# An attention stage with 16 small heads: values made once and spread over DRAM, two-bank scores, outputs issued behind scores

## The chip, the cores and the metric

The kernel runs on one core of one Trainium2 chip. The metric is the device time of one execution in microseconds (us). The kernel before was run three times: 1251.08, 1251.42 and 1253.64 us, median 1251.42 us.

## What is computed

The input is x of 4 sequences of 1024 tokens of 128 features. Two blocks follow each other, each with an attention part and a feed-forward part behind a modulated layer norm. Block 0 has a linear attention and a mixture of 16 small experts. Block 1 has the attention that the change is about, and then a two-layer local transformer as its feed-forward part ("block 2" below). Block 1's attention, shortened:

```python
H, W, PREFIX = 16, 64, 16                  # 16 heads of 8 features
qc = q.reshape(B, H, C, W, 8)              # chunks of 64 queries
kt, vt = the 128 keys and values that end with each chunk (zeros ahead of the start)
sg = einsum('bhcqd,bhkd->bhcqk', qc, k[:, :, :PREFIX]) / sqrt(8)
st = einsum('bhcqd,bhckd->bhcqk', qc, kt) / sqrt(8)
mg = arange(PREFIX) <= q_pos
mt = (diff >= 0) & (diff < W) & (kt_pos >= PREFIX)        # diff = q_pos - kt_pos
scores = concatenate([where(mg, sg, -1e9), where(mt, st, -1e9)], -1)
out = einsum('bhcqk,bhckd->bhcqd', softmax(scores, -1), concatenate([vg, vt], 3))
x = x + ga * (out_as_tokens @ w_out.T)
```

So each query sees the 16 prefix keys and the last 64 keys.

## The kernel before

Activations are kept transposed (`xT`, `hT`: 128 features on the partitions, 1024 tokens along the row), one tile for each of the four sequences b. Block 1's attention works on tiles of 128 queries, 8 for each sequence, 32 in all. A query block has 32 queries and sees three key blocks of 32 (96 keys) and the prefix, so a row has 4 heads x 112 = 448 scores in one PSUM bank, and 4 banks (j = 0 to 3) hold the 16 heads.

For one tile the steps are:

- `scores` (L249): for each of the 4 banks a bf16 matmul writes the mask (identity times the mask constants `mks`, L255); 16 matmuls add the window scores, of which four run on separate row groups of the array (L261); 4 add the prefix scores (L270).
- `weights` (L713): on VectorE (DVE) the negated maximum of each bank (`maximum`, L279) and, for banks 0 to 2, an add of it (L722); on ScalarE (ACT) the exponential. Bank 3 is read by ACT straight from PSUM, one exponential for each head with the maximum as bias (L726). Each bank's result is an SBUF tile `pr`.
- `flip` (L728): TensorE (PE) transposes the 4 heads of a bank into a PSUM tile of tag "t" (two buffers), ACT copies it to SBUF (`pt`, L735).
- `values` (L692): GpSimd (POOL) copies the four overlapping windows of `hT` and the prefix into `hr`; four fp32 matmuls project them (L708), ACT copies the result to `vb`, with a column of ones behind each head's 8 values.
- `outputs` (L739): 64 small matmuls into one half of the bank `obank` (L750, columns 0 to 143 for even tiles, 144 to 287 for odd ones), then on DVE the reciprocal of the sums (`rs`, L752) and the product (`on`, L754).
- `back` (L757): PE transposes `on` into the last 128 columns of the same bank (L760), ACT copies it to `os` (L763).

An fp32 matmul is two instructions in the profile, so 32 instructions on L261 are 16 matmuls.

PSUM has eight banks and all are used: "s" four (scores; block 0's `hidden` uses the same four), "t" two, "m" one (`values`, and in turn `queries`, `keys`, `tokens`, `normed`, `project_out`), "o" one (`obank`).

PE's instructions run in the order in which the program writes them; the other engines' are put in order by the planner ahead of the run, by the order of the program and by when it expects each to be ready. It also sets all waits. The loop over g (from -1 to 33, L792) is that written order: in step g it issues scores and weights of tile g+2, side work (`queries`, `tokens`, `normed` of some sequence), `back` of g-1, the first flip of g+1, values of g+1, outputs of g, the second flip of g+1, and in some steps `project_out`, `keys` and, from g = 26 on, the first projections of block 2 (L651). `tokens` transposes half a sequence into "m" and computes a layer norm's statistics, `normed` transposes it back and writes `hT`.

Block 0's `hidden` (L483) makes two products `h` of 512 columns for each pair of experts; ACT takes the first through silu (`u`), POOL multiplies `u` by the routing weights, DVE multiplies by the second (`g`); `mixed` sums the experts' outputs.

The weights of block 2 (L601 to L613) are loaded by DMAs on SyncE's (SP's) queue at the start of block 1's attention.

Of the kernel before, what the change touches and what calls it, by code (L numbers as in the profile page):

```python
# [19 lines left out]
F32 = mybir.dt.float32  # L20
# [6 lines left out]
P = 128  # L27
# [6 lines left out]
H0 = 16  # L34
# [14 lines left out]
def adaln_blocks(ctx: ExitStack, tc: tile.TileContext, a: dict, out: bass.AP):  # L49
# [199 lines left out]
    def scores(b, t):  # L249
        nt = f"{b}_{t}"  # L250
        q1, kx, kg = kept1[b, "q"], kept1[b, "kx"], kept1[b, "kg"]
        S = [ps.tile([P, 512], F32, tag="s", name=f"s_{nt}_{j}", bufs=4) for j in range(4)]
        sv = [x[:, 0 : 4 * (W3 + PREFIX)].rearrange("p (h k) -> p h k", h=4) for x in S]
        for j in range(4):
            pe.matmul(sv[j], lhsT=identb, rhs=mks[:, min(t, 1), :].unsqueeze(1).to_broadcast([P, 4, W3 + PREFIX]), start=True, stop=False)  # L255
        for a in range(4):
            i = 4 * t + a
            lo = max(0, 2 - i)
            for j in range(4):
# [6 lines left out]
                    stop=False,  # L266
                )
        for j in range(4):
            rw = slice(32 * j, 32 * j + 32)
            pe.matmul(sv[j][:, :, W3:], lhsT=q1[rw, t * P : (t + 1) * P], rhs=kg[rw, 4 * j : 4 * j + 4, :], start=False, stop=True)  # L270
        mx = pre.tile([P, H0], F32, tag="mx", name=f"mx_{nt}", bufs=3)
        kept1[b, t, "s"] = sv, mx
        if (b, t) == (0, 0):
            for j in range(4):
                maximum(b, t, j)

    def maximum(b, t, j):
        sv, mx = kept1[b, t, "s"]
        dve.tensor_reduce(mx[:, 4 * j : 4 * j + 4], sv[j], AX.X, ALU.max, negate=True)  # L279


# [3 lines left out]
    with (  # L285
# [184 lines left out]
        def shared_hidden(b):  # L470

            hh = []
            for i in range(2):
                h = ps.tile([P, BLK], F32, tag="s", name=f"hs{i}_{b}", bufs=4)
                for k in range(NB):
                    pe.matmul(h[k * INTER : (k + 1) * INTER, :], lhsT=ws13[:, i, :], rhs=hT[b][:, blk(k)], start=True, stop=True)
                hh.append(h)
            u = wp.tile([P, BLK], F32, tag="u", name=f"us_{b}")
            act.activation(u, hh[0], AF.Silu)
            g = kept[b, "gs"] = wb.tile([P, BLK], F32, tag="gs", name=f"gs_{b}")  # L480
            dve.tensor_tensor(g, u, hh[1], ALU.mult)

        def hidden(b, k, c):  # L483

            nm = f"{b}_{k}_{c}"
            hh = []
            for w in (w1, w3):
                h = ps.tile([P, BLK], F32, tag="s", name=f"h_{nm}", bufs=4)
                pe.matmul(h, lhsT=w[:, c * P : (c + 1) * P], rhs=hT[b][:, blk(k)], start=True, stop=True)  # L489
                hh.append(h)  # L490
            u = wp.tile([P, BLK], F32, tag="u", name=f"u_{nm}")
            act.activation(u, hh[0], AF.Silu)  # L492
# [3 lines left out]
            dve.tensor_tensor(g, u, hh[1], ALU.mult)  # L496
# [104 lines left out]
    wl = []  # L601
    for l in range(DEPTH):
        w = [const1(f"wqkv_{l}", [P, 3, HEADS * DH]), const1(f"wo_{l}", [P, 4, D]), const1(f"w1_{l}", [P, 2 * HID]), const1(f"w2_{l}", [P, 3, D])]
        nc.sync.dma_start(out=w[0], in_=a["wqkv"][l].rearrange("p (i c) -> p i c", i=3))
        nc.sync.dma_start(out=w[1], in_=a["wo"][l].rearrange("(c p) d -> p c d", p=P))
        nc.sync.dma_start(out=w[2], in_=a["mw1"][l])
        for j, r in enumerate(CH):
            nc.sync.dma_start(out=w[3][:r, j, :], in_=a["mw2"][l][j * P : j * P + r, :])
        wl.append(w)

    abs_ = [const1(f"ab_{l}", [P, 2, NT, 2, DH]) for l in range(DEPTH)]
    tab = abs_[DEPTH - 1]
    nc.sync.dma_start(out=tab, in_=a["tab"])  # L613
# [70 lines left out]
    with (  # L684
        tc.tile_pool(name="w6o", bufs=1) as wo6,
# [4 lines left out]
        odd.append(wo6)  # L690

        def values(b, t):  # L692

            nt = f"{b}_{t}"
            hr = wp.tile([P, 4, KV], F32, tag="hr", name=f"hr_{nt}", bufs=2)
            c0 = 2 if t == 0 else 0
            win = hT[b][:, (4 * t + c0 - 2) * KB :]
            win = bass.AP(tensor=win.tensor, offset=win.offset, ap=[win.ap[0], [KB, 4 - c0], [1, W3]])
            pool.tensor_copy(hr[:, c0:, 0:W3], win)
            if t == 0:  # L700

                pool.memset(hr[:, 0:2, 0 : 2 * KB], 0.0)
# [519 lines left out]
```

## Time and profile before

| | |
|---|---|
| median of three runs | 1251.42 us |
| span of the profiled execution | 1254.1 us |
| its total beside the span | not given apart |
| PE, DVE, ACT, POOL busy in the span | 1167.7, 879.4, 812.7, 812.2 us |
| granted TensorE clock, mean | 0.977 |
| first scores of block 1 (L255) | 324.70 us |
| masks of g = 1 and of g = 26 start | 346.92, 539.03 us |
| first work of block 2 behind the stage (L843) | 588.78 us |

The block 1 attention is thus the stretch from about 325 to 589 us. A line of the profile's timeline gives the start, the time from the first start to the last end of a merged group, engine, line of the kernel, operation, what is written and read, the shapes and the count, and in brackets how long the engine stood idle before it and whom it waited for. Instructions on one engine overlap: what a group costs is the distance from its start to the next group's start. PE is matmul time, PEld the loading of weights, which runs beside it.

### The profile page before, as it was taken

To read this page: it belongs to the slowest core of one execution; us is meant where nothing else is said; L and a number is where in the kernel's file an instruction comes from. 1 tells how busy PE (TensorE), PEld (TensorE's weight loads), DVE (VectorE), ACT (ScalarE), POOL (GpSimd) and SP (SyncE) were. 2 spreads that over 40 slices of the span, in tenths; PEclk is the share of its full clock that TensorE was granted. 3 is DMA by queue.
4 is the path that set the end of the run, shared out by engine and by line. 5 is a ranking of instruction groups with operands and counts; after the bars stand their busy time and mean duration, and the time that the engine had idled before them with its cause. 6 is when DMAs were issued, how large, how long until landed. Compare 5 with 4: busy or idle time off the path is not lost.

```text
span 1254.1 us, 34759 instructions
## 1 busy us (share of the span) xinstructions
PE 1167.7 (93%) x13578; PEld 717.7 (57%) x13578; DVE 879.4 (70%) x2806; ACT 812.7 (65%) x2215; POOL 812.2 (65%) x805
## 2 busy tenths in 40 slices
PE   6788989998899999988898999999999999999998
PEld 5544444543476667665565555656655556566564
DVE  5656263452466666675879888888899888898864
ACT  3362362322477677775787777788878777788862
POOL 4445443745434353534789988988889889888840
PEclk9798999998999999999999999999999999999999
DMA  6040403022300000000111111111111111111110
GB/s 177 1 137 1 137 0 117 20 70 66 135 4 4 3 20 4 20 4 3 27 36 40 26 39 27 35 39 27 39 27 26 39 30 40 48 27 31 36 39 26
DMA packets 36136, 51.04 MB, mean 41 GB/s; under 512 B 5850, under 2 KB 17668, under 8 KB 35844
## 3 DMA queue, kind: packets, MB, share of 16 engines
q1 hardware_dynamic: 35540, 48.29, 14.3%
q8 instruction: 107, 1.75, 0.6%
q10 hardware_dynamic: 432, 0.53, 0.1%
q14 instruction: 57, 0.47, 0.1%
HBM read 26.52 MB, written 2.36 MB: 23 GB/s over the span
## 4 chain that ended last, share of the span: by engine, by line
PE 44%; DVE 25%; ACT 18%; POOL 6%; issue 6%; DMA 1%; POOLq 0%; ACTq 0%; SPq 0%; DVEq 0%
PE h L489 4%; ACT pr L902 4%; PE yp L949 4%; DVE pr L890 4%; DVE co L656 3%; DVE si L661 3%; PE s L883 3%; DVE ss L663 3%; PE ptr L733 3%; POOL u L494 3%; PE qk L651 3%; PE y L504 2%; PE s L261 2%; ACT sq L654 2%; PE obank L750 2%
## 5 line engine op out<-in xcount | busy, mean ns | idle before, releaser
L902 ACT ACTIVATE pr<-pr,mx 128x128 f32<-128x128 f32 x512 | 200.8, 403 | 87.8 <-DVE mx L890 87.7
L671 POOL TENSOR_TENSOR co<-co,si 128x512 f32<-128x512 f32 x123 | 156.5, 1278 | 80.3 <-DVE si L661 73.5
L667 POOL TENSOR_TENSOR ss<-ss,nhalf 128x16 f32<-128x16 f32 x64 | 191.2, 2987 | 5.3
L890 DVE CUSTOM_DVE_ANT_0 pr<-s,masks,ss 128x128 f32<-128x128 f32 x512 | 144.2, 345 | 42.2 <-PE s L883 40.9
L494 POOL TENSOR_TENSOR u<-u,cw 128x512 f32<-128x512 f32 x64 | 81.0, 1268 | 102.3 <-ACT u L492 100.0
L651 PE MATMUL qk<-wqkv,hs 128*128 128x512 f32 x256 | 137.7, 620 | 4.3 <-ACT pt L735 4.3
L496 DVE TENSOR_TENSOR g<-u,h 128x512 f32<-128x512 f32 x64 | 43.9, 686 | 127.2 <-POOL u L494 127.2
L489 PE MATMUL h<-hT,w 128*128 128x512 f32 x256 | 125.0, 612 | 0.4 <-DVE g L496 0.4
L279 DVE TENSOR_REDUCE mx<-s 128x4 f32<-128x448 f32 x128 | 73.6, 618 | 55.2 <-PE s L270 55.2
L492 ACT ACTIVATE u<-h 128x512 f32<-128x512 f32 x64 | 38.2, 597 | 112.8 <-PE h L489 111.3
L656 DVE TENSOR_TENSOR co<-qk,ab 128x512 f32<-128x512 f32 x128 | 87.1, 680 | 26.1 <-ACT sq L654 26.1
L902 ACT ACTIVATION_READ_ACCUMULATOR pr<-pr,mx 128x1 f32 x512 | 101.6, 198 | 0.0
L924 PEld LDWEIGHTS ptr<-ident,pr 128*128 128x128 f32 x512 | 63.6, 141 | 61.6 <-issue 55.1
L661 DVE TENSOR_TENSOR si<-qk,ab 128x512 f32<-128x512 f32 x128 | 87.0, 680 | 0.0
L663 DVE TENSOR_REDUCE ss<-sq 128x8 f32<-128x512 f32 x128 | 86.4, 675 | 0.0
L489 PEld LDWEIGHTS h<-hT,w 128*128 128x128 f32 x256 | 49.8, 198 | 63.8 <-issue 56.7
L654 ACT ACTIVATE sq<-qk 128x512 f32<-128x512 f32 x128 | 74.9, 585 | 14.7 <-PE qk L651 12.2
L843 PE MATMUL qktr<-ident,co 128*128 128x128 f32 x492 | 77.4, 281 | 6.6 <-POOL co L673 5.2
L883 PEld LDWEIGHTS s<-kT,qT 64*64 64x64 f32 x2048 | 56.1, 133 | 45.5 <-issue 22.1
L917 POOL TENSOR_TENSOR pr<-pr,sm 128x512 f32<-128x512 f32 x64 | 74.6, 1167 | 7.8 <-DVE sm L910 7.8
L735 ACT COPY pt<-ptr 112x512 f32<-112x512 f32 x128 | 72.6, 612 | 10.7 <-PE ptr L733 10.7
L883 PE MATMUL s<-kT,qT 64*64 64x128 f32 x2048 | 71.4, 275 | 7.6 <-DVE kT L856 6.1
(211 smaller groups left out, 2865.0 us busy)
## 6 DMA issues: line engine op xcount, KB each, us to landing
cw<-cd SPq DMA_DIRECT2D x128, 128.0 KB, 3.1
ve<-vs SPq DMA_DIRECT2D x120, 128.0 KB, 2.3
hs<-hT SPq DMA_DIRECT2D x16, 256.0 KB, 3.2
out<-out SPq DMA_DIRECT2D x7, 256.0 KB, 2.7
xin<-in_x SPq DMA_DIRECT2D x3, 512.0 KB, 6.1
w<-in_w SPq DMA_DIRECT2D x3, 512.0 KB, 5.9
wqkv<-in_wqkv SPq DMA_DIRECT2D x2, 768.0 KB, 5.3
ab<-in_tab SPq DMA_DIRECT2D x1, 1024.0 KB, 7.0
```

The costliest lines, as they stand in the source:

```text
L489: pe.matmul(h, lhsT=w[:, c * P : (c + 1) * P], rhs=hT[b][:, blk(k)], start=True, stop=True)
L494: pool.tensor_tensor(u, u, kept[b, k, "cw"][:, c, :], ALU.mult)
L651: pe.matmul(ps, lhsT=hs[l, b][:, t * P : (t + 1) * P], rhs=wl[l][0][:, w, :], start=True, stop=True)
L654: act.activation(sq, ph, AF.Square)
L656: dve.tensor_tensor(co, ph, abs_[l][:, 0, t, w, :].unsqueeze(1).to_broadcast([P, HEADS, DH]), ALU.mult)
L661: dve.tensor_tensor(si.rearrange("p h (i e) -> p h i e", i=2), ex, sn, ALU.mult)
L663: dve.tensor_reduce(ss[:, w, :], sq, AX.X, ALU.add)
L667: pool.tensor_tensor(ss, ss, nhalf[:, 0:2].unsqueeze(2).to_broadcast([P, 2, HEADS]), ALU.pow)
L671: pool.tensor_tensor(co, co, si, ALU.add)
L883: pe.matmul(S[j][qs, c, :], lhsT=q[rw, c, qs], rhs=k[rw, c, at : at + P], start=True, stop=True)
L890: dve.tensor_tensor_reduce(out=pr[:, c, :], in0=S[j][:, c, :], in1=mk[:, min(t, 1), :], scale=kept[l, b, t, "ss"][:, 0, h : h + 1], scalar ...
L902: act.activation(pr[:, c, :], pr[:, c, :], AF.Exp, bias=mx[:, j, c : c + 1], scale=-1.0, accum_out=sm[:, j, c : c + 1])
```

## The change

- `values` projects each token once (one matmul of 128 tokens for a tile), ACT copies it with the column of ones to `vt`, and DMAs on SP write it to a DRAM tile `dv`, read the four overlapping windows back into `vb` and the prefix rows four times. Zeros stand ahead of a sequence's start. It is issued two tiles ahead of `outputs`, not one.
- Masks are written to the first and third key block only (256 of 448 columns), except for the first tile of a sequence.
- Scores lie in two tiles of two banks. Banks 2 and 3 come first; DVE takes one maximum over two banks, one add for banks 0 and 1 together (`prw`), and one add for bank 2; ACT does bank 3's exponentials before the others.
- In the loop, `outputs` of g and the flip of banks 3 and 2 come straight behind the scores, ahead of side work; `back`, `values` and the flip of banks 0 and 1 follow.
- Block 0's `hidden` and `shared_hidden` take one two-bank tile where they took two one-bank tiles.
- Block 2's weights are loaded one piece a step, behind the window's DMA, from g = 1 on.

```diff
     def scores(b, t):
-        S = [ps.tile([P, 512], F32, tag="s", name=f"s_{nt}_{j}", bufs=4) for j in range(4)]
-        sv = [x[:, 0 : 4 * (W3 + PREFIX)].rearrange("p (h k) -> p h k", h=4) for x in S]
-        for j in range(4):
-            pe.matmul(sv[j], lhsT=identb, rhs=mks[:, min(t, 1), :].unsqueeze(1).to_broadcast([P, 4, W3 + PREFIX]), start=True, stop=False)
+        S = [ps.tile([P, 2, 512], F32, tag="s", name=f"s_{nt}_{i}", bufs=2) for i in range(2)]
+        sp = [x[:, :, 0 : 4 * KV].rearrange("p j (h k) -> p j h k", h=4) for x in S]
+        sv = [sp[j // 2][:, j % 2] for j in range(4)]
+        for j in (2, 3, 0, 1):
+            to, of = sv[j], mks[:, min(t, 1), :]
+            if t == 0:
+                of = of.unsqueeze(1).to_broadcast([P, 4, KV])
+            else:
+                to = to[:, :, 0:W3].rearrange("p h (c k) -> p h c k", k=KB)[:, :, 0:3:2, :]
+                of = of[:, 0:W3].rearrange("p (c k) -> p c k", k=KB)[:, 0:3:2, :].unsqueeze(1).to_broadcast([P, 4, 2, KB])
+            pe.matmul(to, lhsT=identb, rhs=of, start=True, stop=False)
...
+    def maximum(b, t, i):
+        sp, mx = kept1[b, t, "s"]
+        dve.tensor_reduce(mx[:, 8 * i : 8 * i + 8].rearrange("p (j h) -> p j h", j=2), sp[i], AX.X, ALU.max, negate=True)
...
         def hidden(b, k, c):
-            hh = []
-            for w in (w1, w3):
-                h = ps.tile([P, BLK], F32, tag="s", name=f"h_{nm}", bufs=4)
-                pe.matmul(h, lhsT=w[:, c * P : (c + 1) * P], rhs=hT[b][:, blk(k)], start=True, stop=True)
-                hh.append(h)
+            hh = ps.tile([P, 2, BLK], F32, tag="s", name=f"h_{nm}", bufs=2)
+            for i, w in enumerate((w1, w3)):
+                pe.matmul(hh[:, i], lhsT=w[:, c * P : (c + 1) * P], rhs=hT[b][:, blk(k)], start=True, stop=True)
...
         def values(b, t):
             if t == 0:
+                dv = kept1[b, "dv"] = dr1.tile([2 * KB + N, H0 * 9], F32, tag="dv", name=f"dv_{b}")
+                nc.sync.dma_start(out=dv[0 : 2 * KB], in_=zero)
+            dv = kept1[b, "dv"]
+            vp = ps.tile([P, BLK], F32, tag="m", name=f"vp_{nt}")[:, 0:D]
+            pe.matmul(vp, lhsT=hT[b][:, t * P : (t + 1) * P], rhs=wqkv1[:, 2, :], start=True, stop=True)
+            vt = wp.tile([P, H0, 9], F32, tag="vt", name=f"vt_{nt}")
+            pool.memset(vt[:, :, 8:9], 1.0)
+            act.copy(vt[:, :, 0:8], vp.rearrange("p (h e) -> p h e", e=8))
+            at = 2 * KB + t * P
+            nc.sync.dma_start(out=dv[at : at + P], in_=vt.rearrange("p h e -> p (h e)"))
+            v = kept1[b, t, "v"] = wp.tile([KV, 4, H0 * 9], F32, tag="vb", name=f"vb_{nt}")
+            win = dv[t * P : t * P + W3]
+            win = bass.AP(tensor=win.tensor, offset=win.offset, ap=[win.ap[0], [KB * H0 * 9, 4], win.ap[1]])
+            kept1["brought"] = nc.sync.dma_start(out=v[0:W3], in_=win)
+            nc.sync.dma_start(out=v[W3:KV], in_=dv[2 * KB : 2 * KB + PREFIX].unsqueeze(1).to_broadcast([PREFIX, 4, H0 * 9]))

         def weights(b, t):
-            for j in range(4):
+            wide = kept1[b, t, "pr", 0] = wp.tile([P, 2, 4, KV], F32, tag="prw", name=f"prw_{b}_{t}", bufs=2)
+            for i in (1, 0):
                 if (b, t) != (0, 0):
-                    maximum(b, t, j)
+                    maximum(b, t, i)
+                mi = mx[:, 8 * i : 8 * i + 8].rearrange("p (j h) -> p j h", j=2)
+                if i == 0:
+                    dve.tensor_tensor(wide, sp[0], bc(mi, [P, 2, 4, KV]), ALU.add)
+                    act.activation(wide, wide, AF.Exp)
+                    continue
+                pr = [wp.tile([P, 4, KV], F32, tag="pr", name=f"pr_{b}_{t}_{j}", bufs=4) for j in range(2)]
+                for h in range(4):
+                    act.activation(pr[1][:, h, :], sp[1][:, 1, h, :], AF.Exp, bias=mi[:, 1, h : h + 1])
+                dve.tensor_tensor(pr[0], sp[1][:, 0], bc(mi[:, 0], [P, 4, KV]), ALU.add)
+                act.activation(pr[0], pr[0], AF.Exp)
...
             when(g + 2, scores)
             when(g + 2, weights)
+            when(g, outputs)
+            when(g + 1, flip, (3, 2))
             if ahead and t in (2, 4):
                 queries(b + 1, t // 2 - 1)
...
             when(g - 1, back)
+            for i in {-1: (0, 1)}.get(g, (g + 2,)):
+                when(i, values)
             when(g + 1, flip, (0, 1))
-            when(g + 1, values)
-            when(g, outputs)
-            when(g + 1, flip, (2, 3))
+            if g > 0 and local_loads:
+                with tc.issue_after(kept1["brought"].ins):
+                    nc.sync.dma_start(out=local_loads[0][0], in_=local_loads[0][1])
+                del local_loads[0]
```

## The prediction

> **What bounds the kernel now.** I read the page first, then a table of stages, then the instructions of one step in order of time, then the waits. The page says that TensorE is busy nearly always, and the stage in question is no exception:
>
> ```profile
> PE 1167.7 (93%) x13578; PEld 717.7 (57%) x13578; DVE 879.4 (70%) x2806; ACT 812.7 (65%) x2215; POOL 812.2 (65%) x805
> 450.00:520.00 70.00, 67.09 (x1850) 48.51 (x1848) 47.18 (x113) 50.12 (x124) 35.78 (x59) 1.00 0.05 11
> ```
>
> The second line is a stretch in the middle of block 1's attention (stretch, its length, then busy us of PE, PEld, DVE, ACT, POOL, granted clock, DMA share, GB/s): PE 67.1 of 70 us, DVE 47, ACT 50, clock full, DMA idle. So PE work that goes away should shorten the step, up to the point where a chain through DVE or ACT is as long. One step without side work (g = 15) in the timeline of PE:
>
> ```profile
> 458.61 0.92 PE L255 MATMUL s<-cb,identb 128*128 128x448 bf16 x4
> 459.46 0.93 PE L261 MATMUL s<-kx,q 32*32 32x384 f32 x32
> 460.32 0.47 PE L270 MATMUL s<-kg,q 32*128 32x64 f32 x8
> 460.72 0.33 PE L760 MATMUL obank<-ident,on 128*128 128x128 f32 x1
> 460.88 1.04 PE L733 MATMUL ptr<-ident,pr 128*112 128x128 f32 x8
> 461.75 1.04 PE L708 MATMUL vp<-wqkv,hr 128*112 128x128 f32 x8
> 462.72 1.26 PE L750 MATMUL obank<-vb,pt 112*32 112x9 f32 x128
> 463.91 1.09 PE L733 MATMUL ptr<-ident,pr 128*112 128x128 f32 x8
> 464.83 0.73 PE L255 MATMUL s<-cb,identb 128*128 128x448 bf16 x3
> ```
>
> Start to start this costs: masks 0.85, windows 0.86, prefix 0.40, `back` 0.16, first flip 0.87, values 0.97, outputs 1.19, second flip 0.92; 6.22 in all, no gap. DVE in the same step:
>
> ```profile
> 460.79 1.16 DVE L279 TENSOR_REDUCE mx<-s 128x4 f32<-128x448 f32 x2 [1.91 <-PE s L270]
> 461.86 1.15 DVE L722 TENSOR_TENSOR pr<-s,mx 128x448 f32<-128x448 f32 x2
> 462.92 1.15 DVE L279 TENSOR_REDUCE mx<-s 128x4 f32<-128x448 f32 x2
> 463.98 0.62 DVE L722 TENSOR_TENSOR pr<-s,mx 128x448 f32<-128x448 f32 x1
> 464.51 0.25 DVE L752 RECIPROCAL rs<-obank 128x16 f32<-128x16 f32 x1
> 464.80 0.29 DVE L754 TENSOR_TENSOR on<-obank,rs 128x128 f32<-128x128 f32 x1
> ```
>
> To be seen: DVE starts as soon as the scores are done, does all seven big operations of `weights` (0.53 each, start to start), and only then `rs` and `on` of `outputs`, because `weights` is earlier in the program. `on` ends 4.37 us after PE left the scores (460.72). Nobody minds now: `back` uses `on` one step later.
>
> Two more pairs of lines matter. At the end of the stage:
>
> ```profile
> 582.61 0.26 ACT L763 COPY os<-obank 128x128 f32<-128x128 f32 x1
> 583.01 1.17 PE L750 MATMUL obank<-vb,pt 112*32 112x9 f32 x102 [0.82 <-ACT os L763]
> ```
>
> The outputs of tile 31 write columns 144 to 287 of the bank `obank`; the copy of tile 30 reads columns 384 to 511. They share no element, and still PE waited 0.82 us for the copy: accesses of two engines to one bank are put in program order. And:
>
> ```profile
> 468.06 0.78 ACT L161 ACTIVATE hT<-out_h,mod 128x512 f32<-128x512 f32 x1 [1.38 <-PE out_h L160]
> 468.88 0.93 PEld L708 LDWEIGHTS vp<-wqkv,hr 128*112 128x112 f32 x8 [0.19 <-ACT hT L161]
> ```
>
> The bank "m" exists once: values wait until ACT has emptied it of the side work (here `normed`). Now that is just hidden by a flip and an idle ACT.
>
> **The change, part by part.** *Values once.* 8 matmul instructions of 0.11 to 0.13 us become 2: 0.97 goes to 0.22, 0.75 less PE. ACT's copy of 512 columns (0.60) becomes 128 columns (0.26 by L763), POOL's copies go. Added per tile are three DMAs on SP. The nearest rows: a store to DRAM of 32 KB lands in 1.6 us, a load of 128 KB from it in 3.1, an issue takes 0.35 to 0.6 us of SP. So about 6 to 6.5 us from ACT's copy to the values. They are made two steps ahead, which leaves some 9: hidden, with 2 to 3 us to spare. Spreading 18 weight loads puts at most one of about 6 us behind each step's loads; block 2 needs the first at g = 26. Nothing.
>
> *Masks.* 256 of 448 columns; 0.85 goes to 0.49 if time follows columns (bounds 0.49 and 0.85). Windows need 0.86 and 0.40 as before, so scores take 1.75.
>
> By PE alone a plain step would go from 6.22 to 6.22 - 0.75 - 0.36 = 5.1, some 30 us over the stage. I don't expect that, because of the order.
>
> *Outputs behind scores.* The new order on PE is scores(g+2), outputs(g), flip (3,2), side work, back(g-1), values(g+2), flip (0,1). Now `back`(g-1) comes *after* outputs(g) in the program, and both are in `obank`: `back` writes the bank that `rs` and `on` of tile g read. By the 0.82 us row above it must wait for them, and DVE does them after `weights`(g+2). A wait of the same kind that is 2 us of cover away now (`outputs` behind `os`) is exchanged for one with none.
>
> [...] By address alone `back` would not wait, and the step would be the 5.2 of the first rival below; by the bank it is the 6.97 that follows.
>
> *Two-bank scores.* An operation on 448 columns costs 0.53, start to start. From L754 (128 columns, 0.29) to L656 (512 columns, 0.68) a column costs 1.0 ns, so 448 more add 0.46; on 896 I take 1.0. DVE then has two maxima 1.0, one add 0.53, one add 1.0, `rs` and `on` 0.29 each: 4.1. It can start 0.2 sooner, since banks 2 and 3 are finished first: 0.13 before PE leaves the scores. So `on` ends 3.97 after, and `back` starts at 4.02.
>
> *The new loop*, from PE leaving the scores: wait until 4.02, `back` 0.11, values 0.22, flip 0.87, scores 1.75: **6.97 us for any step**. PE's outputs, flip and side work (1.19 + 0.87 + up to 0.97 = 3.0) all fit inside the wait. On ACT, the exponentials of bank 3 start at 1.0 (4 x 0.235), then two flip copies and an exponential (0.48 each) until 3.4, then the copy that frees "m" (0.58 to 0.78): 4.0 to 4.2, about when `back` is due; 0.1 more with `normed`.
>
> *The sum over g = 1 to 25.* Before: masks start at 346.92 (g = 1) and 539.03 (g = 26), 192.1 us. The step g = 11 took 12.14 where its twin g = 19 took 7.52 (a stall of 1.94 "issue" and slow matmuls after it), and g = 14 has 1.63 of "issue"; without these 185.8. After: 25 x 6.97 = 174.3; six `project_out` of 0.86 behind the loop 5.2; six `keys` of 0.97, 5.8; three of them behind a `project_out`, whose add they await for about 1.0 as now, 3.0; eight `normed` 0.8. Together 189.1, or **+3.3**. So plain steps lose 0.4 to 0.8 (6.22 and 6.62 now), steps with `tokens` 0.3 (6.65), those with `queries` win 0.2 (7.15), those with `normed` stay (7.0 to 7.25).
>
> *Elsewhere.* Steps 26 to 29 carry block 2's first projections; DVE is their limit now (9.0 to 9.4 each) and does the same work: 0. Tail: after the last scores, 20.7 us now; values go (-1), but three `back`s wait for DVE behind the projections' 2.0 us: **+1** (-1 to +2). Head: scores(1) and (2) get their banks some 2 us sooner, then outputs(0) wait for their values to come over DRAM: **-1** (-3 to +1). Block 0: `hidden` now needs both banks free, so its first matmul waits for `g` of two before, not only for `u`. In the trace that `g` is done in time for all but a handful of 62, by which 1.8 us would be lost: **+1** (0 to +2).
>
> Sum +3.3 + 1 - 1 + 1 = +4.3. The profiled execution has a span of 1254.1, which is 2.7 over the median of the three runs and 0.5 over the slowest; its own total is not given apart from the span. I add the sum to the median: 1255.7, rounded 1255.5.
>
> **The rivals.** *Faster: `back` finds `on` ready*, because DVE does `rs` and `on` between its big operations, or no wait is set between columns of one bank. This decides if `on` ends before about 3 us. Then ACT's flip copies rule the plain step: the second flip needs the "ptr" buffers emptied, at 2.5 and 3.0, ends at 3.45, and with scores the step is 5.2, PE's own work; steps with side work still wait for "m" until 4.0 (7.0). Five steps gain 1.75: -9 against my sum, 1246.5. If ACT also empties "m" ahead of an exponential (3.4 instead of 4.0), side steps fall to about 6.4: twenty times 0.6 more, 1234.5. PE's floor (-30, 1221) would need all waits gone. For it: DVE puts other work between `rs` and `on` (an `xh` at 458.05), so its order isn't rigid. Against it: in every step that I read, `rs` follows all of `weights`. Chance 0.35, typically 1240.
>
> *Slower still: ACT does the wide exponential before the copy that frees "m".* Both become ready within 0.1 us (3.47 and 3.41), and the order is fixed ahead of the run. Then values start at 5.0, not 4.2, in the 20 steps with side work: +16, 1271. Chance 0.12.
>
> *The change doesn't do what it says: masks on strided columns cost as before*, 0.85: +0.36 in 28 steps, 1265. The row of 0.21 per 448 columns doesn't tell. Chance 0.05. *Values come late*: if write and read take over 9 us, each step waits for the excess, +1 us a step or 1280. Chance 0.03.
>
> **How the numbers follow.** My case has 0.45, with an own range of 1249 to 1262: a tenth of a us on the loop is 2.5 us, and I hold it to 0.2, beside the bounds of head, tail and block 0. The first rival reaches down to 1221, but mostly lies above 1234; the others lie between 1262 and 1280. Leaving out a tenth on each side gives 1235 to 1270. About 0.2% (2.5 us) is what a measurement of this kernel can tell from no change. Faster: 0.31 of the first rival and 0.04 of mine, 0.35. Within: 0.04 and 0.11, 0.15. Slower: 0.30 of mine and the other three, 0.50.
>
> **What would show it.** Right: `back` (obank<-ident,on) heads PE's waits with "DVE on" at 1 to 2 us in nearly every step; PE's busy time in the stage falls by some 30 us with no gain in time; masks start every 7.0 us. Wrong: masks starting every 5.2 us in plain steps; PE waiting for an ACT copy ahead of `vp`; DVE's `rs` lying among the maxima; outputs waiting for a DMA.

## The result, and the profile after

| | before | after |
|---|---|---|
| median, six runs each | 1254.39 us | 1291.45 us |
| ratio after to before, 95% interval | | 1.0278 (1.0245 to 1.0311) |
| span of the profiled execution (total of after's: 1293.60) | 1254.1 us | 1291.9 us |
| first scores of block 1 | 324.7 us | 321.3 us |
| masks of g = 1, of g = 26 | 346.9, 539.0 us | 345.7, 565.7 us |
| masks of the last tile; first work of block 2 behind the stage | 566.0, 588.8 us | 598.5, 624.6 us |

The changed kernel is slower by 2.8%, 35 us by the ratio and 37 by the medians; I had forecast 4 and a range up to 1270. From the table, the 37.8 us between the spans come from: block 0 -3.4, head of the stage (first scores to g = 1) +2.2, steps g = 1 to 25 +27.8, g = 26 to 28 (masks of g = 26 to masks of g = 29, the last tile) +5.9, tail +3.3, the rest of the kernel +2.0.

Lines of the page of the changed kernel (busy time, share and instructions; the granted clock in tenths over 40 slices; queue 8, which the page names "instruction": packets, MB, share):

```profile
PE 1156.6 (90%) x13386; PEld 705.9 (55%) x13386; DVE 874.7 (68%) x2710; ACT 797.0 (62%) x2181; POOL 787.5 (61%) x730
...
PEclk9798999999898999988899999999999999999999
...
q8 instruction: 106, 1.74, 0.6%
```

The stretch in the middle of the stage, as it was shown for the kernel before (PE, PEld, DVE, ACT, POOL, clock, DMA share, GB/s):

```profile
450.00:520.00 70.00, 56.83 (x1692) 40.30 (x1680) 42.15 (x75) 42.98 (x108) 25.12 (x34) 0.95 0.28 74
```

PE was busy for 67.1 of these 70 us and is now for 56.8. So PE lost work, as the change says, and waits more than it lost. DMA went from 11 to 74 GB/s, and the granted clock from 1.00 to 0.95.

The timeline of PE in step g = 22:

```profile
532.94 0.92 PE L263 MATMUL s<-cb,identb 128*128 128x448 bf16 x4
533.79 0.93 PE L269 MATMUL s<-kx,q 32*32 32x128 f32 x32
534.65 0.45 PE L279 MATMUL s<-kg,q 32*128 32x64 f32 x8
535.03 1.26 PE L762 MATMUL obank<-vb,pt 112*32 112x9 f32 x128
536.22 1.09 PE L745 MATMUL ptr<-ident,pr 128*112 128x128 f32 x8
537.14 0.60 PE L787 MATMUL in_h<-ident,xT 128*128 128x128 f32 x4
539.32 0.33 PE L772 MATMUL obank<-ident,on 128*128 128x128 f32 x1 [1.58 <-DVE on L766]
539.48 0.39 PE L708 MATMUL vp<-wqkv,hT 128*128 128x128 f32 x2
539.71 1.04 PE L745 MATMUL ptr<-ident,prw 128*112 128x128 f32 x8
540.58 0.60 PE L263 MATMUL s<-cb,identb 128*128 128x256 bf16 x4
541.11 0.93 PE L269 MATMUL s<-kx,q 32*32 32x384 f32 x32
541.97 0.47 PE L279 MATMUL s<-kg,q 32*128 32x64 f32 x8
542.36 1.26 PE L762 MATMUL obank<-vb,pt 112*32 112x9 f32 x128
```

and DVE beside it:

```profile
535.13 2.09 DVE L290 TENSOR_REDUCE mx<-s 128x8 f32<-128x896 f32 x2 [1.23 <-PE s L279]
537.14 0.25 DVE L764 RECIPROCAL rs<-obank 128x16 f32<-128x16 f32 x1
537.44 0.62 DVE L735 TENSOR_TENSOR pr<-s,mx 128x448 f32<-128x448 f32 x1
537.98 1.08 DVE L729 TENSOR_TENSOR prw<-s,mx 128x896 f32<-128x896 f32 x1
538.98 0.28 DVE L766 TENSOR_TENSOR on<-obank,rs 128x128 f32<-128x128 f32 x1
```

This is the forecast loop. PE leaves the scores at 535.03; DVE does everything of `weights` and only last `on`, which ends at 539.26; `back` (L772) starts at 539.32. From leaving the scores: `back` after 4.29, then 0.16, values 0.23, flip 0.87, scores 1.78, which is 7.33. `rs` moved between the maxima and the adds, which I had named as a sign of being wrong, but it gained nothing: `on` stayed last. The waits of PE over the stage (us in total, times, longest):

```profile
PE obank L772 <- DVE on L766: 37.8, 26, 2.3
PE obank L762 <- issue: 8.9, 4, 3.1
PE ptr L745 <- issue: 5.8, 3, 2.2
```

The second and third line are stalls for which the profile shows nothing to wait for: 14.8 us, where the kernel before had 5.0. One of them, in step g = 8:

```profile
409.24 1.19 PE L762 MATMUL obank<-vb,pt 112*32 112x9 f32 x120
412.53 0.29 PE L762 MATMUL obank<-vb,pt 112*32 112x9 f32 x8 [2.10 <-issue]
412.76 1.96 PE L745 MATMUL ptr<-ident,pr 128*112 128x128 f32 x8
...
418.88 1.06 PE L263 MATMUL s<-cb,identb 128*128 128x256 bf16 x4
```

PE stops for 2.10 us in the middle of the outputs. The flip behind it takes 1.96 where it took 1.09; the granted clock is 0.50 from 411.69 to 421.93. The step takes 11.43 us (407.45 to 418.88). Pieces at half clock between the first scores and block 2's first work add up to 52.5 us, to 3.4 before.

### The profile page after: what moved, and what is told of

Same layout as the page of the kernel before. It is cut to its first block, busy times and chain, and to the rows that moved or that the text cites. A ratio compares the mean times of both kernels' runs of the same rounds, so it can differ in the third digit from the quotient of the medians.

```text
span 1291.9 us, 34282 instructions
## 1 busy us (share of the span) xinstructions
PE 1156.6 (90%) x13386; PEld 705.9 (55%) x13386; DVE 874.7 (68%) x2710; ACT 797.0 (62%) x2181; POOL 787.5 (61%) x730
## 3 DMA queue, kind: packets, MB, share of 16 engines
q8 instruction: 106, 1.74, 0.6%
## 4 chain that ended last, share of the span: by engine, by line
PE 19%; DVE 18%; ACT 12%; issue 1%; POOL 1%; DMA 0%; DVEq 0%; ACTq 0%; POOLq 0%
ACT pr L919 4%; PE yp L966 4%; DVE pr L907 3%; PE s L900 3%; DVE co L661 3%; DVE si L666 3%; DVE ss L668 3%; PE qk L656 2%; DVE ge L1012 2%; ACT sq L659 2%; PE o L955 2%; ACT ge L1005 2%; PE qktr L860 1%; DVE kT L873 1%; PE ptr L941 1%
## 5 line engine op out<-in xcount | busy, mean ns | idle before, releaser
L656 PE MATMUL qk<-wqkv,hs 128*128 128x512 f32 x256 | 141.9, 637 | 0.4 <-ACT pt L747 0.3
L290 DVE TENSOR_REDUCE mx<-s 128x8 f32<-128x896 f32 x64 | 66.8, 1085 | 75.5 <-PE s L279 75.5
L734 ACT ACTIVATE pr<-s,mx 128x112 f32<-128x112 f32 x128 | 34.9, 355 | 91.5 <-DVE mx L290 86.3
L659 ACT ACTIVATE sq<-qk 128x512 f32<-128x512 f32 x128 | 74.9, 585 | 16.4 <-PE qk L656 13.3
```

The lines of the kernel that those rows point to most:

```text
L656: pe.matmul(ps, lhsT=hs[l, b][:, t * P : (t + 1) * P], rhs=wl[l][0][:, w, :], start=True, stop=True)
L659: act.activation(sq, ph, AF.Square)
```

## The experiments

Ratios are to the kernel before, with 95% intervals; "plain" steps have no side work. Waits and half clock come from one profiled execution each.

### Is it the bank? `back` elsewhere

*e1_back_other_bank*: `back` writes a buffer of tag "t" in place of `obank`.

```diff
-            tp, on = obank[0][:, BLK - P :], kept1.pop((b, t, "o"))
+            on = kept1.pop((b, t, "o"))
+            tp = ps.tile([P, 4, P], F32, tag="t", name=f"bk_{b}_{t}", bufs=2)[:, 0, :]
```

> The kernel after, with one edit: the transpose in `back` goes into a tile of tag "t" instead of the last columns of `obank`; its place in the program is unchanged. Theory A (the wait for the bank, then the clock): `back` of g-1 waits for `rs` and `on` of g only because they read the same bank. In another bank it needs `on` of g-1 alone, which is a step old. PE's wait for `on` (37.8 us in the kernel after) falls below 5 us, plain steps go from 7.3 to about 5.8 us, the half-clock stretches (about 61 us between 325 and 630) become rarer, and the time falls to 1262 to 1275. Rival B (the two-bank chain through DVE and ACT is 7.3 us long wherever `back` stands): PE waits elsewhere for as long, mostly for ACT's copies out of "t" and "m", masks still start every 7.2 to 7.4 us, 1285 to 1295.

*e2_back_first*: `back` of g-1 ahead of the outputs of g.

```diff
             when(g + 2, weights)
+            when(g - 1, back)
             when(g, outputs)
...
-            when(g - 1, back)
```

> The kernel after, with `back` of g-1 moved ahead of `outputs` of g, straight behind the scores; same bank. Theory A: `on` of g-1 is old, so `back` waits for nothing; `outputs` now wait about 0.5 us for ACT's copy `os` (the bank rule the other way round), with ACT idle at that point. Plain steps about 5.8 to 6.0 us, steps with side work 7.0 to 7.4 because "m" is emptied by ACT at about 4.2 us; 1262 to 1278. Rival B: 1285 to 1295.

*e5_side_work_first*: side work and `back` ahead of the outputs; outputs, flip (3,2), values, flip (0,1) follow.

```diff
-            when(g, outputs)
-            when(g + 1, flip, (3, 2))
             (side work)
             when(g - 1, back)
+            when(g, outputs)
+            when(g + 1, flip, (3, 2))
```

> The kernel after, with the order scores, side work, `back`, `outputs`, flip (3,2), values, flip (0,1): side work and `back` stand where they stood in the kernel before, the rest as in the kernel after. Theory A: side work reaches ACT while it is idle (its exponentials start 1.3 us behind the scores), "m" is free again long before values, `back` waits for nothing; plain steps 5.8, side steps 6.2 to 6.6 us; 1235 to 1255, as fast as the kernel before or faster. Rival B: no shorter than 7.2 a step, 1285 to 1295.

Measured: e1 1279.95 us (1.0233, 1.0197 to 1.0268), e2 1278.43 (1.0247, 1.0176 to 1.0317), e5 1303.19 (1.0413, 1.0374 to 1.0452). In e1 and e2 the 37.8 us of `back` are gone from the list, and the step g = 15 fell to 6.28 and 6.47. So the wait was for the bank. But little time was regained, 6 us in e1 and 4 in e2 by the ratios: nearly all steps with side work stayed at 7.3 to 7.7 and more, and e1's steps g = 1 to 25 took 218.9 us, where the changed kernel's took 219.9. e1's waits, of the steps with `normed`, `tokens` and `queries`:

```profile
PE vp L708 <- ACT hT L161: 9.0, 8, 1.3
PE vp L708 <- ACT xt_h L790: 8.9, 8, 1.1
...
PE vp L708 <- ACT q L226: 4.9, 6, 1.1
```

That is the one bank "m", which ACT empties behind its exponentials: a second chain that is nearly as long, because values lie directly behind the side work. This is my first rival's case as I wrote it (7.0 with side work), only somewhat longer. In e1, g = 26 to 28 took 7.71, 10.16 and 8.24, to 9.98, 12.46 and 10.43 in the changed kernel: 6.8 of the 15.1 us between the two profiled executions, the largest part. e5 missed its expectation; it shows a wait on the same bank the other way round, 45.2 us in 31 times:

```profile
PE obank L762 <- ACT os L775: 45.2, 31, 2.6
```

Side work delays `back`, its copy to `os` falls behind bank 3's exponentials on ACT, and the outputs, which write other columns of the bank, wait for that copy.

### Does the loop run through the scores, and is the low clock the price?

*e14_full_masks*: all 448 mask columns again.

```diff
-            if t == 0:
-                of = of.unsqueeze(1).to_broadcast([P, 4, KV])
-            else:
-                (strided, 256 columns)
+            of = of.unsqueeze(1).to_broadcast([P, 4, KV])
```

> The changed kernel with masks on all 448 columns again, 0.32 us more of PE for each of 28 tiles. Theory A (the step is a loop that runs through the scores, the masks among them): plain steps go from 7.32 to 7.64 us, as the tiles with full masks already have, and the time rises by 7 to 9 us to 1297-1301 us. Rival (PE has waits enough to hide it): no change, 1288-1294 us.

*e3_filler*: two useless transposes ahead of each real four in flip (3,2), so that PE stands less idle.

```diff
+                if j > 1:
+                    for h in range(2):
+                        pe.transpose(tp[:, h, :], ident[:, 0:KV], ident)
```

> The kernel after, with work added: two more transposes (of the identity, overwritten by the real ones) ahead of those of bank 3 and of bank 2 in each tile, 8 more PE instructions of 0.11 us a step, 0.87 us of matmul that stands ahead of the wait for `on`. Order and waits are as they were. Theory A's second half (idle PE loses its clock): PE idles 0.9 us less in each step, so it is at half clock for much less than 61 us between 325 and 630; clean steps stay at 7.3, and the time falls by 5 to 20 us although 28 us of work are added, 1272 to 1287. Rival C (the slow steps come from instruction fetch or DMA traffic, and the low clock only follows them): half-clock time as before, time the same or up to 10 us longer, 1290 to 1302.

Measured: e14 1297.72 (1.0342, 1.032 to 1.0363); plain steps 7.64. So 0.32 us more of PE between `back` and the end of the next scores cost 0.31 a step, although PE waits elsewhere in the step. e3 1290.08 (1.0312, 1.028 to 1.0343): time at half clock fell from 52.5 to 15.5 us, the time didn't. `back` still waited 30.6 us. So most of the low clock comes with PE's idle time here; what it costs by itself I can't separate, since the filler itself lengthened many steps by 0.3.

### The order alone: outputs back between the flips

*e4_outputs_between*: as the changed kernel, but in the order of the kernel before (scores, side work, `back`, flip (3,2), values, outputs, flip (0,1)).

```diff
             when(g + 2, weights)
-            when(g, outputs)
-            when(g + 1, flip, (3, 2))
             (side work)
             when(g - 1, back)
+            when(g + 1, flip, (3, 2))
             for i in {-1: (0, 1)}.get(g, (g + 2,)):
                 when(i, values)
+            when(g, outputs)
             when(g + 1, flip, (0, 1))
```

> The changed kernel with the outputs put back between the flips (scores, side work, back, flip of heads 3 and 2, values, outputs, flip of heads 0 and 1), as the kernel before had them; two-bank scores, values over DRAM and masks stay. Theory A (the wait of `back` for the copies of `on` is the loop's price): it goes, since `back` then runs before the vector engine comes to `rs` and `on` of the same step; the plain steps fall from 7.3 to 6.0-6.4 us, and the time to 1240-1262 us. Rival B (the two-bank scores themselves are the price: the outputs then wait for the output copies, which stand behind the exponentials of the second bank): steps stay at 6.9 us or more, a wait of the outputs for `os` shows over 25 us, and the time stays above 1270 us. Theory E (the bare stalls of PE come from scores and outputs directly behind each other): with the flip between them, PE's stalls put down to issue fall from 14.7 to about 5 us.

*e6_back_last*: values and outputs behind the scores, then flip (3,2), side work, flip (0,1), and `back` last.

```diff
             when(g + 2, weights)
+            for i in {-1: (0, 1)}.get(g, (g + 2,)):
+                when(i, values)
             when(g, outputs)
             when(g + 1, flip, (3, 2))
             (side work)
-            when(g - 1, back)
-            (values)
             when(g + 1, flip, (0, 1))
+            when(g - 1, back)
```

> The changed kernel with the values (two ahead) and the outputs directly behind the scores as changed, then flip of heads 3 and 2, the side work, flip of heads 0 and 1, and `back` last. Theory A: `back` now comes some 3 us later in the step, when `on` has long been copied, and the side work lies before it with a whole flip between it and the next wait, so plain and side steps fall to 6.2-6.6 us and the time to 1238-1258 us. Rival (PE has simply more work, no wait): no change from the changed kernel's 7.3 us and 1290 us. Theory E: the stalls put down to issue stay at 11-15 us or grow, since scores, values and outputs still lie next to each other.

*e12_back_behind_scores*: e4 with `back` directly behind the scores.

```diff
             when(g + 2, weights)
+            when(g - 1, back)
             (side work)
-            when(g - 1, back)
```

> The changed kernel with the outputs between the flips, as in the run e4_outputs_between, and `back` of the tile before moved up to directly behind the scores, ahead of the side work. In e4_outputs_between the outputs waited 15.9 us in 23 steps for `os`, whose copy stood on the scalar engine behind the exponentials of bank 3, because side work delayed `back`. Theory A (one bank rule, both ways round): with `back` directly behind the scores its copy is done before those exponentials begin, `on` of the tile before has been ready since 4.1 us after the scores before; so both waits are short, plain steps stay at 5.3 us, side steps fall from 6.6-6.8 to 6.0-6.3, and the time is 1232-1244 us, below the kernel before. Rival: the outputs then wait for the flip copies on the scalar engine instead, or steps are as long for another reason: 1247-1253 us.

Measured: e4 1250.44 (0.9984, 0.9959 to 1.0008), e6 1249.11 (0.9968, 0.995 to 0.9986), e12 1256.08 (1.0014, 0.9991 to 1.0036). e4 differs from the changed kernel in the place of two calls and is some 37 us faster (0.9984 beside 1.0278). Its plain step has no gap:

```profile
449.16 0.60 PE L263 MATMUL s<-cb,identb 128*128 128x256 bf16 x4
449.69 0.93 PE L269 MATMUL s<-kx,q 32*32 32x384 f32 x32
450.54 0.47 PE L279 MATMUL s<-kg,q 32*128 32x64 f32 x8
450.94 0.33 PE L772 MATMUL obank<-ident,on 128*128 128x128 f32 x1
451.11 1.04 PE L745 MATMUL ptr<-ident,pr 128*112 128x128 f32 x8
451.98 0.39 PE L708 MATMUL vp<-wqkv,hT 128*128 128x128 f32 x2
452.30 1.26 PE L762 MATMUL obank<-vb,pt 112*32 112x9 f32 x128
453.49 1.09 PE L745 MATMUL ptr<-ident,prw 128*112 128x128 f32 x8
454.41 0.80 PE L263 MATMUL s<-cb,identb 128*128 128x256 bf16 x4
```

5.25 us, the 5.2 that PE's work alone was to give. In steps with side work the same kernel still pays:

```profile
PE obank L762 <- ACT os L775: 15.9, 23, 1.5
```

e12 removes that (0.7 us left, once), its undisturbed side steps take 5.95 to 6.12 as I had expected, and yet it is not faster: stalls put down to issue and pieces at half clock grew to 16.4 and 34.1 us (e4: 9.6 and 20.5). My expectation of 1232 to 1244 missed. The profiled execution of e12 was one of its slowest (1263.47, of 1249.92 to 1263.47), so the stall sums overstate the median. e6 beats the kernel before by 0.3%, and it keeps the outputs and the first flip ahead of the side work, as the change does. So it is not their early place alone that costs, but how soon `back` and values follow: in e6 `back` waited 3.2 us for `on`, not 37.8, and values waited 0.4 us for "m".

### One bank or two

*e8_one_bank*: the kernel before with the values over DRAM (and block 2's weights spread) and the masks on two blocks; scores and order stay.

```diff
-            when(g + 1, values)
+            for i in {-1: (0, 1)}.get(g, (g + 2,)):
+                when(i, values)
```

> The kernel before with two parts of the change alone: values projected once, two tiles ahead, and spread by DMA over DRAM, and masks on two of three key blocks; scores in one pool's order as before, outputs between the flips. Theory A (the order of outputs and `back` is what costs, values and masks are harmless or a small gain): 1243-1252 us, at or up to 8 us below the kernel before, with the steps still bound by the wait of the scores for the bank that flip and exponentials release (6.4 us a step). Rival C (the spread by DMA or the added mask product is the price): 1260 us or more, with waits of PE for the DMA of `vb` or longer scores.

*e13_one_bank_new_order*: e8 with the changed order.

```diff
             when(g + 2, weights)
+            when(g, outputs)
+            when(g + 1, flip, (0, 1))
             (side work)
             when(g - 1, back)
-            when(g + 1, flip, (0, 1))
             (values)
-            when(g, outputs)
             when(g + 1, flip, (2, 3))
```

> The run e8_one_bank (scores in single banks, values over DRAM, masks on two blocks) with the changed order in the loop: outputs and the first flip directly behind the scores, `back` behind the side work. Theory A (order alone is the price): `on` ends 4.4 us after the scores, so a step is 4.4 + 0.11 + 0.22 + 0.87 + 1.75 = 7.4 us or more, PE's waits are headed by `back` for `on` with over 30 us, and the time is 1285-1305 us. Rival B (the two-bank scores are needed for the loss): the time stays below 1265 us.

Measured: e8 1251.74 (0.999, 0.9973 to 1.0007), with 14.0 us of scores waiting for bank 3's exponentials in 18 steps; e13 1347.34 (1.0736, 1.071 to 1.0761). With the kernels above this makes a square: in the old order two banks or one make no difference that shows (e4, e8); the new order costs 94 us with one bank (1.0736 beside 0.999) and 37 with two. So the order as a whole is the price, and the two-bank scores soften it. e13 lost more than I expected:

```profile
PE obank L768 <- DVE on L762: 34.6, 23, 2.3
PE vp L709 <- ACT xt_h L785: 10.5, 8, 2.1
PE vp L709 <- ACT hT L161: 8.3, 6, 2.0
PE vp L709 <- ACT q L226: 8.2, 6, 2.2
```

To the wait for `on` comes the one for "m", 27 us, and pieces at half clock of 117 us in all. How much of the excess each of these is, the runs don't tell.

### Where do the bare stalls come from?

*e11_weights_in_bulk*: the changed kernel, block 2's weights loaded at once at the start.

```diff
+    for to, of_ in local_loads:
+        nc.sync.dma_start(out=to, in_=of_)
...
-            if g > 0 and local_loads:
-                with tc.issue_after(kept1["brought"].ins):
-                    nc.sync.dma_start(out=local_loads[0][0], in_=local_loads[0][1])
```

> The changed kernel with block 2's weights loaded all at once at the start instead of spread over block 1's steps, so that no such transfer lies beside the attention loop. Theory D (PE's bare stalls are instruction fetches that collide with transfers): stalls put down to issue fall from 14.7 to about 5 us in the stage, and the time by about 8 us to 1283 us. Theory E (they come from how dense short instructions lie): the stalls stay at 12-16 us and the time at 1288-1294 us.

*e15_before_with_traffic*: the kernel before plus the value transfers, to a tile nobody reads.

```diff
+            with tc.issue_after(came.ins):
+                nc.sync.dma_start(out=dv[2 * KB + t * P : 2 * KB + t * P + P], in_=still)
+            nc.sync.dma_start(out=vs[0:W3], in_=win)
+            nc.sync.dma_start(out=vs[W3:KV], in_=(prefix rows, four times))
```

> The kernel before with the change's value traffic added and read by nobody: in each step, behind the copy of the values, a 72 KB store to DRAM, a load of the four windows (216 KB) and of the prefix rows (36 KB). Theory D (PE's bare stalls, put down to issue, and the low clock behind them come from transfers that delay the fetching of PE's instructions): stalls in the stage grow from 5.0 to 10-15 us, and the time by 5-15 us to 1259-1269 us. Theory E (they come from how densely PE's short instructions follow each other): the stalls stay at about 5 us and the time at 1252-1257 us.

*e16_no_traffic*: e12 without the transfers; it leaves out the spreading of values, and all tiles use the first tile's.

```diff
+            if "vb" in kept1:
+                kept1[b, t, "v"] = kept1["vb"]
+                return
```

> The run e12_back_behind_scores without the transfers in the loop: all tiles use the first tile's values (this leaves out the values' spreading, so outputs are of wrong values), and block 2's weights are loaded in bulk at the start. All of PE's instructions stay. Theory D: stalls put down to issue fall from 16.4 to about 5 us, time at half clock from 34 to under 15 us, and the time by 10-15 us to 1240-1246 us. Theory E: stalls stay at 10-16 us and the time within 4 us of 1256.

*e17_fewer_instructions*: e12 with one product for each head in place of four; all four query blocks use the first one's window, the other three are left out.

```diff
-                    for c in range(4):
-                        qs = slice(c * KB, (c + 1) * KB)
-                        pe.matmul(o[qs, 4 * j + h, :], lhsT=pt[:, h, qs], rhs=v[:, c, ...], start=True, stop=True)
+                    pe.matmul(o[:, 4 * j + h, :], lhsT=pt[:, h, :], rhs=v[:, 0, ...], start=True, stop=True)
```

> The run e12_back_behind_scores with one product for each head in `outputs` in place of four (16 matmuls a tile, not 64; all four query blocks use the first block's window, so three quarters of the outputs are of wrong keys). PE's instructions for outputs fall from 128 to 32 matmul instructions a tile; PE's time falls by about 0.9 us a step. Theory E: stalls put down to issue fall from 16.4 to under 5 us. Theory D: they stay above 10 us. By either the time falls, by 20-30 us where PE's work sets the step, by less than 10 us where chains over the scalar and vector engine do.

Measured: e11 1292.05 (1.0318, 1.0291 to 1.0345), stalls 10.8 us, no gain; e15 1258.4 (1.0052, 1.0029 to 1.0074); e16 1241.14 (0.9922, 0.9893 to 0.995); e17 1352.32 (1.0801, 1.077 to 1.0832). The waits of PE in e12:

```profile
PE obank L762 <- issue: 8.7, 5, 3.1
PE ptr L745 <- issue: 6.6, 3, 3.2
```

and in e16, the same lines of PE's program:

```profile
PE ptr L753 <- issue: 2.4, 3, 1.2
...
PE obank L770 <- issue: 1.3, 2, 0.7
```

Without transfers, stalls fall from 16.4 to 3.9 us, half clock from 34.1 to 10.2, and the time by 12 us by the ratios, 15 by the medians. The stalls are from one profile each, but they agree over all kernels: the four without transfers beside the loop (before, e16, e18, e19) have 2.6 to 5.5 us, those with them and with all outputs 5.9 to 16.4. So the transfers add to the stalls, though not always much: e5 has 5.9 us, and e15 6.4 to the 5.0 before, with 0.5% more time. e15's transfers did not spread over all steps: its stores were all issued by 376 us, and the transfers ran at 78 to 133 GB/s until some 465 us (g = 16). In e17, with all transfers in place but outputs thinned out, there is not one stall.

What PE waits for I infer from the traces. Queue 8 carries 1.74 MB in 106 packets of 16 KB in the changed kernel, one for each 253 of PE's 26772 matmuls and weight loads; e17 has 6144 of these fewer and 24 packets fewer. If one numbers PE's recorded instructions from the start of the program, all 128 stalls in block 1's attention, in 17 of the 18 kernels, lie at the same place of a run of 256 (number 193 or 194), and PE goes on 1.2 to 1.6 us after a packet of queue 8 has landed. In the step g = 8 above, the packet ran from 409.94 to 411.34, and PE went on at 412.53. From these counts I take the bare stalls for PE waiting for its own instructions; no record of the traces names that wait. A tile's outputs are 256 of them within 1.19 us; e17 needs 10.7 us or more for such a run of 256 in this stage, e12 as little as 3.0. How the transfers add to the wait stays open: a packet takes as long with them (median 1.1 us in e12) as without (1.1 in e16).

e17's time is another matter; I had expected it to fall. Its outputs in one step:

```profile
454.87 3.64 PE L760 MATMUL obank<-vb,pt 112*128 112x9 f32 x32
```

32 instructions with 128 stationary columns take 3.5 us start to start, 0.11 each, where 128 with 32 columns take 1.19, 0.0093 each. A quarter of the instructions took three times as long. The weight load of one took 192 ns (median at full clock), to 109 in the changed kernel.

### What is left of the change

*e18_without_values*: the order of e12, two-bank scores and masks, but values as in the kernel before.

```diff
-            for i in {-1: (0, 1)}.get(g, (g + 2,)):
-                when(i, values)
+            when(g + 1, values)
```

> The changed kernel without the values' detour: values projected four times from copied windows, one tile ahead, as in the kernel before; block 2's weights in bulk at the start; `back` directly behind the scores, outputs between the flips (the order of e12_back_behind_scores); two-bank scores and masks on two of three blocks stay. No transfers lie beside the attention loop. Theory (both: order and traffic were the price): PE's work bounds the step, 6.22 - 0.32 = 5.9 us for plain steps and 6.7-6.8 with side work; stalls put down to issue under 6 us in the stage; 1238-1246 us, below the kernel before. Rival (two-bank scores cost more than they give): 1250 us or more, with waits of PE for exponentials or flip copies.

*e19_masks_alone*: the kernel before with the masks on two of three blocks.

```diff
+                to = to[:, :, 0:W3].rearrange("p h (c k) -> p h c k", k=KB)[:, :, 0:3:2, :]
+                of = of[:, 0:W3].rearrange("p (c k) -> p c k", k=KB)[:, 0:3:2, :].unsqueeze(1).to_broadcast([P, 4, 2, KB])
```

> The kernel before with the masks on two of three key blocks alone. If PE's work alone bounds the step, 0.32 us of 28 tiles go: -9 us, 1244 us. If the scores then wait for their banks (the exponentials of bank 3 and the adds release them; in e8_one_bank that wait was 14.0 us in 18 steps), less than half of it is left: 1248-1252 us.

Measured: e18 1257.22 (1.0026, 1.0011 to 1.0042), e19 1248.68 (0.9963, 0.9944 to 0.9982). e18's plain steps take 5.90, as worked out, and its stalls are 5.5 us; but steps with `queries` take 7.91, where the kernel before takes 7.15 and e19 6.83 to 7.37: values await `q`'s copy out of "m" (5.3 us, six times). The expectation missed. The trace shows only part of it: the profiled execution (1253.02) was near the low end of 1251.47 to 1259.84, so where the median loses stays open. e19 beats the kernel before by 0.4% and is as good as e6; the scores give back part of the masks' gain by waiting for their banks (5.5 us, 12 times).

## Why the prediction was wrong, point by point

- **Mechanism: right, but not alone.** `back` waits for `on` behind all of DVE's `weights`, heads PE's waits, and PE's saved time is not gained. But the chain through "m" is nearly as long in steps with side work, so taking the wait away (e1, e2) regains only 4 to 6 of some 35 us; only another order regains all (e4, e6). The wait is for the bank, not for the columns: `back` writes columns 384 to 511, `on` reads 0 to 287, and PE waited 26 times, 37.8 us in all. The opposite order (e5, 45.2 us of waits for the copy `os`) and the other bank (e1, where the 37.8 us are gone) confirm it.
- **The loop, mis-sized: 6.97 forecast, 7.33 measured**, 0.36 in 25 steps, 9.0 us. The largest error is DVE's start: I let it begin 0.13 before PE leaves the scores, since banks 2 and 3 are finished first; it begins 0.10 after. Then 0.04 in DVE's chain, 0.05 in `back`, 0.03 in the scores (masks 0.53, not 0.49). The head start of the two-bank order did not come: the four prefix products of a tile run almost at once (in g = 22 their second halves start within 0.02 us, at 534.81 to 534.83), so banks 2 and 3 are finished only 0.01 us before 0 and 1.
- **Tiles with full masks: forgotten.** 7.64 where nothing else disturbs them (g = 14 and 22), 0.32 more in three steps, 1.0 us.
- **Disturbances: the step that failed most.** I took out the stalls of the kernel before (6.3 us) and put none in after. The shortest form of each step over three kernels with this loop (after, e3, e11) sums to 202.68 us for g = 1 to 25; after took 219.93. So 17.3 us are bare stalls and steps at half clock, 11.0 more than before. With the 9.0, the 1.0 and 3.5 that I can't place, this is the 24.5 us between +3.3 and +27.8. I costed the transfers by whether they come in time (they did: one wait of 1.6 us for `vb`) and not by what they do to others; the bare stalls, which I take for waits of PE for its instructions, are 16.4 us with the transfers in e12 and 3.9 without them in e16.
- **Steps 26 to 28 ("26 to 29" in the forecast): 0 forecast, +5.9 measured.** I called DVE their limit, and read their lengths as 9.0 to 9.4, where they were 8.6, 9.3 and 9.0. It is the same wait for `on` (1.99 and 2.31 us in two of them) and stalls; e1 takes the wait away and 2.2 us a step with it.
- **Tail +3.3 for +1, head +2.2 for -1, block 0 -3.4 for +1, the rest +2.0 for 0.** In block 0 `hidden` does wait for `g` (6.4 us, seven times), yet the stage begins earlier, with less time at half clock ahead of it (34.1 us for 47.8) and shorter waits of PE's `y` for `xT` (4.7 us for 11.3). Untested.
- **The rivals.** The first one's price for a loop without the wait, 5.2, is the plain step of e4; but with the changed order the "m" chain would have held the steps with side work at 7.3 and more, as in e1. The second rival did not occur: ACT copied "m" before the wide exponential in every step with side work (538.70 and 539.17 in g = 22). Masks on strided columns do cost less (0.53 us, not 0.85); values do not come late. The range ended at 1270 because no case of mine had a cost outside the loop's chain; that case was missing.

## What to carry to other kernels

Before work is moved ahead in an engine's program, ask which readers of its PSUM bank then stand between it and the next writer, on which engine they queue, and behind what; here the next writer, `back`, waited 37.8 us for such a reader on DVE. Price new transfers not only by their arrival but also by what runs beside them: the bare stalls of PE in this stage were 16.4 us with the transfers beside the loop (e12) and 3.9 without (e16), and in e17, with the transfers and a quarter of the output instructions, there were none. Ask also whether a chain over another engine closes the loop before TensorE time is saved elsewhere in the step: here PE's busy time fell by 10 of 70 us, and the plain step grew from 6.22 to 7.33.

## What the runs showed of the hardware that I had not expected

- In block 1's attention, over 17 kernels, PE stalled without a releaser at one place in a run of 256 of its instructions, 128 times of 128, until 1.2 to 1.6 us after a 16 KB packet of queue 8 had landed. With the transfers beside the loop (74 GB/s in the changed kernel from 450 to 520 us) such a stall took up to 3.2 us (e12); without them up to 1.2 in e16 and 2.3 in e18.
- In the changed kernel the granted clock fell to 0.5 in seventeen pieces, each of 3.4 us or two, three or five times that. Eleven of them lie in block 1's attention, where no wait of PE was over 3.1 us. And in e17 PE is listed as busy for 67.73 of 70 us, with a clock of 0.78:

```profile
450.00:520.00 70.00, 67.73 (x648) 51.00 (x647) 31.25 (x58) 33.22 (x80) 20.85 (x28) 0.78 0.21 61
```

So a PE that the profile called busy still lost its clock here; its weight loads were busy for 51.00 of the 70 us.

- An fp32 product with 128 stationary columns and 9 moving ones took 0.11 us an instruction from start to start (e17), one with 32 stationary columns, whose outputs go to four groups of 32 partitions in turn, 0.0093 (the changed kernel).
